# Three of seven own products of a pair as float32r parts, in a three-layer graph network on one core

## The chip, the cores and the metric

The kernel runs on one core of a Trainium2 chip. The metric is the device time of one execution in microseconds (us). Before the change it is 458.73 us, the median of three runs (457.68 to 459.39). "Slower" and "faster" are against that median.

## The reference, cut to what matters

```
h = relu(layernorm(x));  xs = [h]
for W, b in ((W0, b0), (W1, b1), (W2, b2)):        # three layers
    m = concat(h[dst], h[src] - h[dst]) @ W + b    # 80,000 edges
    h = relu(segment_sum(m, dst) / max(count, 1))  # 2,500 nodes, 256 columns
    xs.append(h)
out = x + concat(xs) @ Wf + bf
```

The sum over edges can be written with a matrix A of edge counts between nodes. With W = (Wt over Wb), a layer is relu of h·(Wt − Wb) + share·A·(h·Wb) + b, up to a scaling of each row by its count. The first term is called the *own* term here: it takes a node's own row of h and no edge. A second stream adds h·Wf, layer by layer, to the output, which is kept in `acc`.

## The kernel before, in words

**Layer 0** builds A from the edges, group by group of 504 nodes (486 in the fifth), uses it at once and stores it to memory as bf16 (`a_dram0` to `a_dram4`, by transfers of POOL's queue). Its own products are already made from three float32r parts: a float32 number is split into a high part and a low part of 12 bits each, and a third part across them; three products of float32r parts give the product of two float32 numbers. `Forms` splits a weight (steps high, low, across, last), `Split` and `split_own` split node values.

**Layers 1 and 2** have two phases each. First come ten *nodes* steps: h·Wb and h·Wf for two tiles of 128 nodes, again by three float32r parts; `parts` writes the result in a high and a low float32r half (`zh`, `zl`), `combine` and `sums` make four sums of it for the second phase (`sh`, `sl`), and `add_to_acc` adds the Wf part to `acc`. The fifth group (`Alone`) is multiplied beside them. Then comes the *stream*. The four other groups form two pairs, `Pair(l, 0)` and `Pair(l, 1)`. For a pair, the product of a 2×2 arrangement of blocks is made with seven products instead of eight. The seven right sides are `b11`, `b21`, `b22` and the sums `r1 = b11 + b12`, `r2 = r1 + b22`, `r3 = b11 − r2`, `r4 = r2 + b21`. The 20 tiles of A are cut into five *chunks* of four, so a pair is 5 × 7 = 35 *steps*, and a layer's stream is 70 steps, n = 0 to 69. A step is four float32r products of 128x504. I call the chunks of the two pairs chunk 0 to chunk 9.

For every step, `Pair.make` makes a block in float32r from the staged bf16 data: ACT casts `b11`, `b21`, `b22`, `r1`, `r2`; DVE adds `r1` and `r2` in place in bf16 before their casts, and makes `r3` and `r4` itself. The blocks have seven buffers, and `Stream.run` makes a block at most six steps ahead of the step that PE is at. Each chunk's data are two loads of 504 KB on SP's queue into one of four `staged` buffers.

Each of the seven sums in PSUM also gets its own term: one plain float32 product of the seven-products form, with a weight from `ws` (`b11`, `b21`, `r4`) or from the sums `wsum` (`b22`, `r1`, `r2`, `r3`) and with the same right side taken from `hT`. The right sides that are sums are made by `own_sum` in buffers of `tmps` (six). All seven are issued in the last chunk of a pair (`c == Q // 2 - 1`). When a sum is complete, `take` reads it; the last steps write relu of the result to `hT`, which the next layer's nodes read.

The order on each engine is fixed: PEo, DVEo, ACTo, POOLo and SPo keep the order in which the code is written, and each instruction waits by semaphore only for what it needs. So `tick(n)` and the loops in `run` set the order by their step numbers. SP and POOL are queues of their own: a transfer is issued when its own wait is over, whatever step the other engines are at, but not before the transfers ahead of it in its queue.

Names of the text: `acc` (output), `bf_sb` (bf in all partitions), `add_bf` (called at each `r2` that is made, first in chunk 0 of layer 1), `load_alone` (the loads of the fifth group), `coming` (the forms of the next layer's weights).

Of the kernel before, what the change touches and what calls it, by code (L numbers as in the profile page):

```python
# [298 lines left out]
def by_windows(ctx: ExitStack, tc: tile.TileContext, x, src, dst, Ws, bs, Wf, bf, out, missing):  # L299
# [3 lines left out]
    P = 128  # L303
# [694 lines left out]
    def flat(l):  # L998
        return raws[l].rearrange("p c t d -> p c (t d)") if l < L else wfs[l]
# [42 lines left out]
    own_forms, own_parts, bf_sb, blocks = [], {}, [], []  # L1042

    def forms_of_own():
        parts = [hot.tile([P, DC, D], F32R, name=f"own_w{k}", bufs=1) for k in range(3)]
# [39 lines left out]
    class Group:  # L1085
# [32 lines left out]
    def begin():  # L1118
        g = len(now)
        now.append(Group(g, as_[g]))  # L1120
        if g == 0:
            ps.append(ps_right)
            pre.close()
            apools.append(second.enter_context(tc.tile_pool(name="apool1", bufs=1)))
        if g + 1 < NG:
            as_[g + 1] = new_a(g + 1)
            return
        second.close()
        raw_pools.append(ctx.enter_context(tc.tile_pool(name="raw", bufs=1, side="right")))
        bf_sb.append(raw_pools[-1].tile([P, D], F32, name="bf_sb"))  # L1130
        SPo.dma_start(bf_sb[0], bass.AP(tensor=bf.tensor, offset=bf.offset, ap=[[0, P], [1, D]]))
        blocks.append(ctx.enter_context(tc.tile_pool(name="ready", bufs=7, side="right")))

    def each(of):
# [16 lines left out]
    def take_next(it=iter(range(len([b for b in windows if b[0] == 0]), len(windows)))):  # L1151
# [11 lines left out]
        "h": each((late_final, (q,)) for q in LATE),  # L1163
    }
    later = """
        g d d d B18 u G4 u B23 d d u u G2 u B21 d u B24 ws c e e e e B14 B22 B20 b L3 u d d d b b d u u u c d y
        e e o e o b u b c o o e e u e e w e f b c u u b b d e e e e u c b b d d u u u d w e e e e u c d e d d u
        b b c r g u e u e b w e u u c w b b e y e e e d u u p x u u u c d u u u o e e b b f c e e e b b d o p e
        e e e u u u c d d d u u u o u o b e e b e e c e d b b d u d d r g c e u u u e e y u b b u u u c d d u u
        p u u u b e e e c b y d d b b e o f u c b e e o u e u e e e e u u p d c o d o e e e e b c e e e f d b d  # L1170
        b u u u c b b p r b g u u u u c x u o u u e b b o u u u e c e e e e e e p e o x b b e e e u u u c u u b
        b e c e e o e u b s y b c e e e e u e f k v v v v u u l u r g u s u u u u u u p u q o q o u s p u u o u
        q u u q u u u o u u u n n n n h s h x r l
        """
    acts.update(steps)
    for name in (order + later).split():
# [7 lines left out]
    bf_sb = bf_sb[0]  # L1184
    first_layer.close()

    turn_of = [0, 0]
# [8 lines left out]
    def any_bank():  # L1196
# [74 lines left out]
    class Pair:  # L1271

        def __init__(self, l, i):
            self.l, self.i = l, i
            self.one, self.two = (slice(c0, c0 + n) for c0, n in map(group_of, pairs[i]))
            self.bank, self.r = {}, {}
# [7 lines left out]
        def make(self, c, what, st, made):  # L1284
            to = made[what] = block()[:, :, :GS]
            b11, b21, b12, b22 = (st[:, g, h::2, :] for g in range(2) for h in range(2))
            if what[0] == "b":
                ACTo.copy(to, {"b11": b11, "b21": b21, "b22": b22}[what])
            elif what == "r1":
                DVEo.tensor_add(b12, b11, b12)  # L1290
                ACTo.copy(to, b12)
            elif what == "r2":
                DVEo.tensor_add(b22, b12, b22)
                ACTo.copy(to, b22)
            elif what == "r3":
                DVEo.tensor_sub(to, b11, b22)
            else:
                DVEo.tensor_add(to, b22, b21)

        def own_sum(self, i):  # L1300
# [10 lines left out]
            elif i == 3:  # L1311
                r["r4"] = tmp()[:, :GS]
                DVEo.tensor_add(r["r4"], r["r2"], hT[:, 1, one])

        def multiply(self, c, part, what, made):
            if c == 0:
                self.bank[what] = any_bank()[:, :GS]
            to = self.bank[what]
            if c == Q // 2 - 1:
                if part[0] == "x":  # L1320
                    w = ws[self.l][0][:, part[2], part[1] * P:(part[1] + 1) * P]
                else:
                    w = wsum[:, part[1], :]
                m = {"b11": hT[:, 0, self.one], "b21": hT[:, 1, self.one], "b22": hT[:, 1, self.two]}.get(what)
                PEo.matmul(to, w, self.r[what] if m is None else m, start=False, stop=False)
# [82 lines left out]
    class Stream:  # L1408
# [21 lines left out]
        def run(self, tick):  # L1430
            for n, (m, p, c, part, what, made) in enumerate(self.steps):
                self.make(n + LEAD + 1)
                if c == 2:
                    p.own_sum([w for _, w in SEVEN].index(what) - 2)
# [14 lines left out]
    for l in range(1, L):  # L1449
        order = orders[l]  # L1450
        lone = Alone(l, order)
        if l == 1:
            load_alone(0, order)
            split(order[2])
        pending = []
        stream = Stream(l)
        for i in range(Q + LAG):
            if 0 < i <= Q:
                lone.make(i - 1)
            if i < Q:  # L1460
# [12 lines left out]
            if 0 < i <= DC:  # L1473
                lone.own(i - 1, 0)
            if i >= LAG:
                lone.multiply(i - LAG)
            if i == Q - 1:
                load_alone(Q // 2 - 1, order)
                stream.load(3)
        stream.make(2)  # L1480
        lone.end()
        turn_of[1] = 0
        if l + 1 < L:
            load_b(l + 1, SPo)
            load_wb(l + 1, SPo)
            load_wt(l + 1, SPo)
        load_wf(l + 1, SPo)
        after = orders[l + 1]

        def tick(n):  # L1490
            if n == 68 and l + 1 == L:
                begun.append(split_in_blocks(6, False))
            if n == 3:
                combine(wsum, ws[l][0].rearrange("p c (o n) -> p (c o) n", o=2))
            if n == 40 and l + 1 < L:
                DVEo.tensor_sub(ws[l + 1][0], ws[l + 1][0], ws[l + 1][1])
            if n in (49, 56):
                split(after[(n - 49) // 7])
            if n == 63 and l + 1 < L:
                load_alone(0, after)  # L1500
            if n in ((65,) if l + 1 < L else (63, 65)):
                split(after[2 + (65 - n) // 2])
            if n == 64:
                raw = flat(l + 1)
                coming[:] = [Forms(raw, [raw[:, c, :] if l + 1 < L else raws[L][:, c, 0, :] for c in range(DC)])]
                coming[0].high()
                coming[0].low()
            if n == 66:
                coming[0].across()
            if n == 67:  # L1510
                coming[0].last()

        stream.run(tick)

# [76 lines left out]
```

## Time and profile before

| what | value |
|---|---|
| median of 3 runs | 458.73 us (457.68 to 459.39) |
| profiled execution, its own time | 458.63 us |
| its span, first to last instruction | 456.5 us |
| PE busy | 449.2 us, 98% |
| DVE busy | 372.8 us, 82% |
| ACT busy | 318.9 us, 70% |
| granted clock | 1.000 |

The profile is of one execution. Layer 0 is the first 187 us of the span, layer 1's nodes run to about 236 us and its stream to about 312 us, layer 2's nodes to about 361 us and its stream to about 437 us; the last 20 us are h·Wf of layer 2 and the output. In rows of the profile "PEld" is the load of a weight, which overlaps products. A float32 product stands as two records, a float32r product as one. All ordered instructions have the helper's line 267, so groups are told apart by tile names.

### The profile page before, as it was taken

How to read it: one execution, taken by the hardware profiler on the slowest of the kernel's cores; microseconds unless marked ns; L12 is line 12 of the kernel's file. 1: busy time of each engine (PE TensorE's matmuls, PEld its weight loads, DVE VectorE, ACT ScalarE, POOL GpSimd, SP SyncE). 2: the span in 40 equal slices, each digit the busy share in tenths (PEclk: the TensorE clock that was granted, in tenths of full speed). 3: DMA queues.
4: the chain of work that ended last, by engine and by line, in shares of the span. 5: the costliest groups of instructions: out<-in, count | busy, mean ns of one | idle time of the engine just before them, and what ended most of it. 6: DMA issues, size and time to landing. Idle time of an engine off the chain costs nothing.

```text
span 456.5 us, 7452 instructions
## 1 busy us (share of the span) xinstructions
PE 449.2 (98%) x2737; PEld 358.2 (78%) x2737; DVE 372.8 (82%) x724; ACT 318.9 (70%) x586; POOL 43.6 (10%) x64
## 2 busy tenths in 40 slices
PE   8999999999999999999999999999999999999996
PEld 4888877888888888878878868867888787688685
DVE  6999999998899555379979859876999687569796
ACT  5898878777764535397779849756877897497540
POOL 4790101101022010100000000000000000000000
PEclk9999999999999999999999999999999999999999
DMA  8310266833719985611495522011124855220015
GB/s 277 115 36 1 51 122 111 157 79 70 151 36 192 154 199 103 145 47 45 123 378 204 182 90 93 0 45 47 46 54 142 326 184 180 90 92 1 1 53 176
DMA packets 22056, 52.47 MB, mean 115 GB/s; under 512 B 1931, under 2 KB 12382, under 8 KB 22014
## 3 DMA queue, kind: packets, MB, share of 16 engines
q1 hardware_dynamic: 14654, 33.83, 22.2%
q0 software_dynamic: 5856, 16.48, 19.0%
q10 hardware_dynamic: 1504, 1.63, 1.1%
q8 instruction: 22, 0.36, 0.3%
q14 instruction: 20, 0.16, 0.1%
HBM read 36.47 MB, written 15.62 MB: 114 GB/s over the span
## 4 chain that ended last, share of the span: by engine, by line
PE 89%; DMA 3%; POOL 3%; DVE 3%; ACT 1%; issue 1%; ACTq 0%; POOLq 0%
PE bank L267 89%; DMA acc<-in_x_dram 2%; POOL acc L267 1%; DMA staged<-a_dram 1%; DVE st L267 1%; POOL es L267 1%; POOL ed L267 1%; DVE acc L267 0%; DVE staged L267 0%; DVE mv L267 0%; ACT block L267 0%; DVE tmp L267 0%; ACT tmp L267 0%; DVE zl L267 0%; ACT zh L267 0%
## 5 line engine op out<-in xcount | busy, mean ns | idle before, releaser
L267 ACT CAST block<-staged 128x1008 fp32r<-128x1008 bf16 x120 | 117.9, 1031 | 18.9 <-DVE staged L267 6.5
L267 PE MATMUL bank<-block,zh 128*128 128x504 f32 (+1 forms) x200 | 83.7, 418 | 0.0
L267 PE MATMUL bank<-a,zh 128*128 128x504 f32 (+1 forms) x200 | 80.3, 401 | 0.0
L267 PE MATMUL bank<-a,zl 128*128 128x504 f32 (+1 forms) x200 | 77.9, 389 | 0.0
L267 PE MATMUL bank<-block,zl 128*128 128x504 f32 (+1 forms) x200 | 77.2, 386 | 0.0
L267 ACT CAST a<-bank 128x480 fp32r<-128x480 f32 (+1 forms) x105 | 53.0, 568 | 26.6 <-PE bank L267 26.6
L267 PE MATMUL bank<-block,sh 128*128 128x504 f32 x160 | 69.1, 432 | 0.0
L267 DVE TENSOR_TENSOR one_m<-iota_m,key_m 128x2048 bf16<-128x2048 bf16 (+2 forms) x55 | 63.9, 1162 | 5.9 <-PE bank L267 5.9
L267 PE MATMUL bank<-block,staged 128*128 128x512 f32 (+1 forms) x288 | 62.8, 369 | 0.2 <-DVE staged L267 0.2
L267 PE MATMUL bank<-block,sl 128*128 128x504 f32 x160 | 62.5, 391 | 0.0
L267 PEld LDWEIGHTS bank<-block,staged 128*128 128x128 f32 x288 | 49.3, 189 | 10.6 <-DVE staged L267 0.8
L267 DVE TENSOR_TENSOR block<-staged 128x1008 fp32r<-128x1008 bf16 x40 | 46.9, 1204 | 5.3 <-PE bank L267 3.9
L267 PEld LDWEIGHTS bank<-block,zh 128*128 128x128 f32 x200 | 37.6, 188 | 10.8 <-issue 2.1
L267 PEld LDWEIGHTS bank<-block,zl 128*128 128x128 f32 x200 | 37.6, 188 | 10.5 <-issue 3.5
L267 PEld LDWEIGHTS bank<-a,zl 128*128 128x128 f32 x200 | 37.7, 188 | 7.4 <-issue 0.5
L267 PEld LDWEIGHTS bank<-a,zh 128*128 128x128 f32 x200 | 37.6, 188 | 7.5 <-issue 0.5
L267 DVE TENSOR_TENSOR one_n<-iota_n,key_n 128x640 bf16<-128x640 bf16 (+2 forms) x110 | 42.7, 429 | 0.0
L267 PEld LDWEIGHTS bank<-block,sh 128*128 128x128 f32 x160 | 30.1, 188 | 10.5 <-issue 3.5
L267 PEld LDWEIGHTS bank<-block,sl 128*128 128x128 f32 x160 | 30.1, 188 | 9.3 <-issue 3.7
L267 DVE TENSOR_TENSOR staged<-staged 128x1008 bf16<-128x1008 bf16 x40 | 27.1, 679 | 12.0 <-ACT block L267 11.6
L267 PEld LDWEIGHTS <-one_m 128*128 128x128 bf16 x834 | 29.1, 98 | 7.3 <-issue 4.3
L267 PE MATMUL bank<-own_w,hT 128*128 128x256 f32 x144 | 34.7, 385 | 0.0
(192 smaller groups left out, 645.2 us busy)
## 6 DMA issues: line engine op xcount, KB each, us to landing
staged<-a_dram SPq DMA_DIRECT2D x52, 504.0 KB
a_dram<-a POOLq DMA_DIRECT2D x20, 630.0 KB, 9.0
acc<-in_x_dram POOLq DMA_DIRECT2D x3, 640.0 KB, 17.2
out_dram<-acc SPq DMA_DIRECT2D x5, 256.0 KB
acc<-in_x_dram SPq DMA_DIRECT2D x2, 512.0 KB
acc<-in_x_dram ACTq DMA_DIRECT2D x1, 768.0 KB
out_dram<-acc SPq DMA_DIRECT2D x5, 128.0 KB
wt<-in_L_gnn_W_dram SPq DMA_DIRECT2D x2, 256.0 KB
```

The lines of the kernel that those rows point to most:

```text
L267: return self.tc.keep_in_program_order(call(*args, **kwargs))
```

## The change

Four things change, in layers 1 and 2.

1. `b11`, `b21` and `r4` get their own term as three float32r products: `own_high` (ACT) and `own_rest` (DVE) split the right side into three `tmps` buffers, and a `Forms` splits the layer's weight into one of the four `staged` buffers (`room`). The other four own products stay plain float32.
2. All own products leave the last chunk where the table `AT` says so: in pair 0, `b22` goes to chunk 1, `b11` and `b21` to chunk 2, `r4` to chunk 3; in pair 1, `b21` goes to chunk 2, `b11` and `r4` to chunk 3. `r1`, `r2`, `r3` (and `b22` in pair 1) stay in the last chunk. The steps at which sums, splits, forms and loads for the next layer are issued move with it; `coming` is begun at step 54 instead of 64 and takes three of the seven block buffers from then on.
3. `r1` is written back to memory in layer 1 (ten transfers of SP's queue, 252 KB each), and layer 2 reads it, so it leaves ten adds of DVE out.
4. `bf` is added by four transfers of POOL's queue that add to `acc`, instead of by four adds of DVE. The load of `bf_sb` falls away.

```
     def add_bf():
+        row = bass.AP(tensor=bf.tensor, offset=bf.offset, ap=[[0, P], [0, 5], [1, D]])
         for t in range(0, NT, 5):
-            DVEo.tensor_add(acc[:, t:t + 5, :], acc[:, t:t + 5, :], bf_sb.unsqueeze(1).to_broadcast([P, 5, D]))
+            POOLo.dma_start(acc[:, t:t + 5, :], row, accum_op=OP.add)
             yield
             yield
...
+    THREE = ("b11", "b21", "r4")
+    OWNS = THREE + ("b22", "r1", "r2", "r3")
+    AT = {
+        "own": ((2, 2, 3, 1, 4, 4, 4), (3, 2, 3, 4, 4, 4, 4)),
+        "sums": ((14, 16, 20, 17), (50, 51, 55, 51)),
+        "high": ((0, 0, 20), (39, 45, 56)),
+        "rest": ((3, 10, 23), (41, 47, 57)),
+        "wsum": 2, "forms": (6, 8, 9, 9), "split": (53, 57, 65, 64), "load": 61,
+        "sub": 39, "coming": (54, 61, 64, 65), "begun": 68,
+    }
...
             elif what == "r1":
-                DVEo.tensor_add(b12, b11, b12)
+                if self.l == 1:
+                    DVEo.tensor_add(b12, b11, b12)
+                    SPo.dma_start(a_dram[pairs[self.i][1]][:, 4 * c:4 * c + 4:2, :], b12)
                 ACTo.copy(to, b12)
...
+        def own_high(self, what):
+            self.threes[what] = [tmp()[:, :GS].bitcast(F32R) for _ in range(3)]
+            ACTo.activation(self.threes[what][0], self.own_of(what), AF.Copy, scale=DOWN)
+
+        def own_rest(self, what):
+            h = self.own_of(what)
+            high, low, across = self.threes[what]
+            DVEo.tensor_sub(low, h, high.bitcast(F32))
+            DVEo.scalar_tensor_tensor(across, low.bitcast(F32), -E12, high.bitcast(F32), op0=OP.mult, op1=OP.add)
+
+        def own(self, to, part, what):
+            if what in self.threes:
+                for k, m in enumerate(self.threes.pop(what)):
+                    PEo.matmul(to, own_forms[-1].parts[k][:, part[2], part[1] * P:(part[1] + 1) * P], m,
+                               start=False, stop=False)
...
-            if c == Q // 2 - 1:
-                if part[0] == "x":
...
+            if c == AT["own"][self.i][OWNS.index(what)]:
+                self.own(to, part, what)
...
         def tick(n):
...
+            if n == AT["wsum"]:
                 combine(wsum, ws[l][0].rearrange("p c (o n) -> p (c o) n", o=2))
+                room = stage.tile([P, 4 * GS], F32R, name="staged")
+                own_forms.append(Forms(ws[l][0], [ws[l][0][:, c, :] for c in range(DC)],
+                                       [room[:, k * DC * D:(k + 1) * DC * D].rearrange("p (c d) -> p c d", c=DC)
+                                        for k in range(3)]))
+            for k, step in enumerate(("high", "low", "across", "last")):
+                if n == AT["forms"][k]:
+                    getattr(own_forms[-1], step)()
```

On PE, where the own product of `b11` stands in the last chunk of pair 0 of layer 1 before:

```order
L267 MATMUL bank<-hT,wt 128x504
L267 MATMUL bank<-block,zh 128x504
L267 MATMUL bank<-block,zl 128x504
L267 MATMUL bank<-block,zh 128x504
L267 MATMUL bank<-block,zl 128x504
L267 MATMUL bank<-hT,wt 128x504
```

And now, in chunk 2 of the same pair (`staged` is here the buffer with the split weight):

```order
L267 MATMUL bank<-tmp,staged 128x504 x3
L267 MATMUL bank<-block,zh 128x504
L267 MATMUL bank<-block,zl 128x504
L267 MATMUL bank<-block,zh 128x504
L267 MATMUL bank<-block,zl 128x504
L267 MATMUL bank<-tmp,staged 128x504 x3
```

One float32 row became three rows of float32r, and the place is two chunks earlier.

On ACT, at the end of chunk 0's casts and through chunk 1's, layer 1. Before:

```order
L267 CAST block_3305<-staged_3256 128x2x504
L267 CAST block_3325<-staged_3259 128x2x504
L267 CAST block_3332<-staged_3259 128x2x504
L267 CAST block_3342<-staged_3259 128x2x504
L267 CAST block_3349<-staged_3259 128x2x504
L267 CAST block_3357<-staged_3259 128x2x504
L267 CAST block_3380<-staged_3262 128x2x504
L267 CAST block_3386<-staged_3262 128x2x504
```

Now (`staged_3342` is `room`, `staged_3254`, `_3257` and `_3260` are chunks 0, 1 and 2):

```order
L267 CAST block_3304<-staged_3254 128x2x504
L267 ACTIVATE tmp_3309<-hT_86 128x504
L267 ACTIVATE tmp_3313<-hT_86 128x504
L267 CAST block_3332<-staged_3257 128x2x504
L267 CAST block_3343<-staged_3257 128x2x504
L267 CAST block_3352<-staged_3257 128x2x504
L267 CAST block_3359<-staged_3257 128x2x504
L267 CAST block_3368<-staged_3257 128x2x504
L267 ACTIVATE staged_3342<-wt_2828 128x512
L267 CAST block_3394<-staged_3260 128x2x504
L267 ACTIVATE staged_3342<-wt_2828 128x256 x4
L267 CAST block_3407<-staged_3260 128x2x504
```

Two high parts went between the casts of chunk 0 and chunk 1, and five instructions on the weight between those of chunk 1 and chunk 2. The first write to `room` also waits for the store of chunk 0's `r1`, since `room` takes chunk 0's buffer.

On SP's queue, from the loads of chunk 2 on, layer 1 now:

```order
L267 DMA staged_3260<-a_dram1_108 128x2016
L267 DMA brow_95<-in_L0_gnn_b2_dram 1x256
L267 DMA wbf_3292<-in_L0_gnn_W2_dram 128x2x256
L267 DMA wt_3293<-in_L0_gnn_W2_dram 128x2x256
L267 DMA wbf_3292<-in_L0_gnn_Wf_dram 128x2x256
L267 DMA a_dram1_108<-staged_3254 128x2x504
L267 DMA staged_3324<-a_dram0_107 128x2016
L267 DMA staged_3324<-a_dram1_108 128x2016
L267 DMA a_dram1_108<-staged_3257 128x2x504
```

The rows are the same before, but for the two stores to `a_dram1`: a store of `r1` stands ahead of each later chunk's loads.

More of the change, by code (lines that the diff above doesn't have):

```diff
@@ L1040, in last @@
                 ACTo.activation(self.parts[2][:, c, :], self.rest[c], AF.Copy, scale=1.0 / C1)
-    own_forms, own_parts, bf_sb, blocks = [], {}, [], []
+    own_forms, own_parts, blocks = [], {}, []
     def forms_of_own():
@@ L1129, in begin @@
         raw_pools.append(ctx.enter_context(tc.tile_pool(name="raw", bufs=1, side="right")))
-        bf_sb.append(raw_pools[-1].tile([P, D], F32, name="bf_sb"))
-        SPo.dma_start(bf_sb[0], bass.AP(tensor=bf.tensor, offset=bf.offset, ap=[[0, P], [1, D]]))
         blocks.append(ctx.enter_context(tc.tile_pool(name="ready", bufs=7, side="right")))
@@ L1165, in by_windows @@
     later = """
[L1166 to L1173, printed above, removed]
+        g d d d B18 u G4 u B23 d d u u G2 u B21 d u B24 ws c e e e e B14 B22 B20 b L3 u d d d b b d u u u c d y e e o e o b u b c o o e e u e e w e f b c u u b b d e e e e u c b b d d u u u d w e e e e u c d e d d u b b c r g u e u e b w e u u c w b b e y e e e d u u p x u u u c d u u u o e e b b f c e e e b b d o p e e e e u u u c d d d u u u o u o b e e b e e c e d b b d u d d r g c e u u u e e y u b b u u u c d d u u p u u u b e e e c b y d d b b e o f u c b e e o u e u e e e e u u p d c o d o e e e e b c e e e f d b d b u u u c b b p r b g u u u u c x u o u u e b b o u u u e c e e e e e e p e o x b b e e e u u u c u u b b e c e e o e u b s y b c e e e e u e f k v v v v u u l u r g u s u u u u u u p u q o q o u s p u u o u q u u q u u u o u u u n n n n h s h x l r
         """
@@ L1183, in by_windows @@
     ps_left = ctx.enter_context(tc.tile_pool(name="ps_left", bufs=4, space=PSUM))
-    bf_sb = bf_sb[0]
     first_layer.close()
@@ L1275, in __init__ @@
             self.one, self.two = (slice(c0, c0 + n) for c0, n in map(group_of, pairs[i]))
-            self.bank, self.r = {}, {}
+            self.bank, self.r, self.threes = {}, {}, {}
         def load(self, c):
@@ L1313, in own_sum, with own_of @@
                 DVEo.tensor_add(r["r4"], r["r2"], hT[:, 1, one])
+        def own_of(self, what):
+            m = {"b11": hT[:, 0, self.one], "b21": hT[:, 1, self.one], "b22": hT[:, 1, self.two]}.get(what)
+            return self.r[what] if m is None else m
+        def own_high(self, what):
[11 more added lines that the diff above has]
+                               start=False, stop=False)
+            elif part[0] == "x":
+                PEo.matmul(to, ws[self.l][0][:, part[2], part[1] * P:(part[1] + 1) * P], self.own_of(what),
+                           start=False, stop=False)
+            else:
+                PEo.matmul(to, wsum[:, part[1], :], self.own_of(what), start=False, stop=False)
         def multiply(self, c, part, what, made):
@@ L1318, in multiply @@
             to = self.bank[what]
-            if c == Q // 2 - 1:
-                if part[0] == "x":
[L1321 to L1325, printed above, removed]
+            if c == AT["own"][self.i][OWNS.index(what)]:
+                self.own(to, part, what)
             for k, j in enumerate((2 * c, 2 * c + 1)):
@@ L1432, in run @@
                 self.make(n + LEAD + 1)
-                if c == 2:
-                    p.own_sum([w for _, w in SEVEN].index(what) - 2)
+                for k in range(4):
+                    if n == AT["sums"][p.i][k]:
+                        p.own_sum(k)
+                for k, own in enumerate(THREE):
+                    if n == AT["rest"][p.i][k]:
+                        p.own_rest(own)
+                    if n == AT["high"][p.i][k]:
+                        p.own_high(own)
                 p.multiply(c, part, what, made)
@@ L1490, in tick @@
         def tick(n):
-            if n == 68 and l + 1 == L:
+            if n == AT["begun"] and l + 1 == L:
                 begun.append(split_in_blocks(6, False))
-            if n == 3:
+            if n == AT["wsum"]:
                 combine(wsum, ws[l][0].rearrange("p c (o n) -> p (c o) n", o=2))
-            if n == 40 and l + 1 < L:
+                room = stage.tile([P, 4 * GS], F32R, name="staged")
[5 more added lines that the diff above has]
+                    getattr(own_forms[-1], step)()
+            if n == AT["sub"] and l + 1 < L:
                 DVEo.tensor_sub(ws[l + 1][0], ws[l + 1][0], ws[l + 1][1])
-            if n in (49, 56):
-                split(after[(n - 49) // 7])
-            if n == 63 and l + 1 < L:
+            if n == AT["load"] and l + 1 < L:
                 load_alone(0, after)
[L1501 to L1511, printed above, removed]
+            for k in range(3 if l + 1 < L else 4):
+                if n == AT["split"][k]:
+                    split(after[k])
+            for k, step in enumerate(("high", "low", "across", "last")):
+                if n == AT["coming"][k]:
+                    if k == 0:
+                        raw = flat(l + 1)
+                        coming[:] = [Forms(raw, [raw[:, c, :] if l + 1 < L else raws[L][:, c, 0, :] for c in range(DC)])]
+                    getattr(coming[0], step)()
         stream.run(tick)
```

## The prediction

> **What bounds the kernel now.** First the page: who is busy, and on whom the chain of waits lies. Then the chain in order of time.
>
> ```profile
> span 456.5 us, 7452 instructions
> PE 449.2 (98%) x2737; PEld 358.2 (78%) x2737; DVE 372.8 (82%) x724; ACT 318.9 (70%) x586; POOL 43.6 (10%) x64
> ...
> PE 89%; DMA 3%; POOL 3%; DVE 3%; ACT 1%; issue 1%; ACTq 0%; POOLq 0%
> ```
>
> ```profile
> 200.00 252.10 PE bank L267 x1094
> 452.10 0.02 issue
> 452.12 0.48 DVE acc L267
> ```
>
> ```profile
> PEld bank L267 <- ACT block L267: 1.5, 8, 0.2
> ```
>
> From 200.00 to 452.10 us the chain is PE alone. Both streams that change lie in it, so a microsecond of PE taken out is one off the end, unless a new wait takes its place. The third view (waits) says how close that is: in the whole run PE's weight loads waited for ACT's casts 8 times, 1.5 us together.
>
> **The own product.** The timeline of PE over the last chunk of pair 0 in layer 1, then layer 0's own products, which are already three float32r parts:
>
> ```profile
> 262.31 1.01 PE L267 MATMUL bank<-hT,wt 128*128 128x504 f32 x2
> ...
> 272.85 1.00 PE L267 MATMUL bank<-tmp,wt 128*128 128x504 f32 x2
> ...
> 274.16 0.39 PE L267 MATMUL bank<-block,zh 128*128 128x504 f32 x1
> ...
> 275.98 0.39 PE L267 MATMUL bank<-block,zh 128*128 128x504 f32 x1
> ```
>
> ```profile
> 96.45 0.62 PE L267 MATMUL bank<-wt,own_w 128*128 128x504 f32 x2
> 96.91 0.39 PE L267 MATMUL bank<-own_h,own_w 128*128 128x504 f32 x1
> ```
>
> Durations overlap, so starts are what counts. Between 274.16 and 275.98 lie 8 float32r products: 0.228 us each, 0.91 a step. Between 262.31 and 272.85 lie 6 steps with an own product: 1.757 each, so a float32 own product costs 0.847. Three float32r products cost 0.68 (by layer 0's rows, 0.46 for two, 0.69). Each replaced product saves 0.16, and there are 3 × 4 pairs = 12: **1.9 us**. The Trainium skill ("FP8 and Floating Point Precision", TensorE Precision Notes) has true FP32 as four passes through the array and reduced precision as one read. By that a quarter of 0.847 would go, 0.21 each or 2.5 us; the rows show each float32r product at 0.228 rather than 0.212, so I keep 1.9 and make the rule a rival.
>
> **What DVE and ACT get.** Groups of both, ACT's first:
>
> ```profile
> L267 ACT CAST block<-staged 128x1008 fp32r<-128x1008 bf16 x120 | 117.9, 1031 | 18.9 <-DVE staged L267 6.5 <-PE bank L267 6.4 <-DVE tmp L267 2.3
> L267 ACT ACTIVATE wt<-hT 128x504 fp32r<-128x504 f32 x6 | 3.7, 624 | 5.2 <-issue 2.6 <-PE bank L267 1.9 <-DVE hT L267 0.6
> L267 ACT ACTIVATE own_w<-wt 128x512 fp32r<-128x512 f32 x1 | 0.7, 653 | 0.0
> L267 ACT ACTIVATE own_w<-wt 128x256 fp32r<-128x256 f32 x4 | 1.5, 450 | 0.7 <-DVE wt L267 0.7
> L267 ACT COPY tmp<-bank 128x504 f32<-128x504 f32 x8 | 4.6, 578 | 16.0 <-PE bank L267 16.0
> L267 ACT ACTIVATE hT<-hT 128x1008 f32<-128x1008 f32 x8 | 8.3, 1044 | 4.4 <-DVE hT L267 4.4
> ```
>
> ```profile
> L267 DVE TENSOR_TENSOR block<-staged 128x1008 fp32r<-128x1008 bf16 x40 | 46.9, 1204 | 5.3 <-PE bank L267 3.9
> L267 DVE TENSOR_TENSOR staged<-staged 128x1008 bf16<-128x1008 bf16 x40 | 27.1, 679 | 12.0 <-ACT block L267 11.6
> L267 DVE TENSOR_TENSOR hT<-bank,tmp 128x504 f32<-128x504 f32 x12 | 8.1, 678 | 6.4 <-PE bank L267 6.4
> L267 DVE TENSOR_TENSOR acc<-acc,bf_sb 128x1280 f32<-128x1280 f32 x4 | 5.9, 1486 | 0.0
> L267 DVE TENSOR_TENSOR wt<-hT,wt 128x504 fp32r<-128x504 f32 x6 | 4.1, 680 | 0.9 <-ACT wt L267 0.9
> L267 DVE SCALAR_TENSOR_TENSOR wt<-own_w,wt 128x256 f32<-128x256 f32 x2 | 0.8, 422 | 0.0
> ```
>
> Per layer ACT gains six high parts (0.62 each) and a weight split (0.65 + 4 × 0.45): 6.2 us. DVE gains 12 × 0.68 for the rests and 4 × 0.42 for the weight: 9.8 us; it loses the four bf adds (5.9) in layer 1 and ten `r1` adds (6.8) in layer 2. None of that is on the chain; it costs only where a cast comes late. Four tight places:
>
> *Start of a stream.* A chunk is 6.4 us of PE.
>
> ```profile
> 237.28 5.69 ACT L267 CAST block<-staged 128x1008 fp32r<-128x1008 bf16 x6
> 243.15 6.83 ACT L267 CAST block<-staged 128x1008 fp32r<-128x1008 bf16 x7 [0.17 <-DVE staged L267]
> ```
>
> ```profile
> 243.93 2.33 DVE L267 TENSOR_TENSOR block<-staged 128x1008 fp32r<-128x1008 bf16 x2
> ```
>
> Six casts take 5.69, so 0.95 each and 4.75 a chunk: 1.65 spare. Chunks 0 to 2 get 1.25 + 2.45 = 3.7 of new ACT work against 3 × 1.65 = 5.0 spare, and 0.85 + 2 × 0.68 of own products now stand there for PE to work on. The two high parts push chunk 1's first cast from 237.28 + 3 × 0.95 = 240.1 to about 241.2; PE is at step 2 when the first of those three casts ends (238.3) and wants step 7 at 242.9. Chunk 1's casts then end near 246.4. The weight follows: its high part to 247.1, DVE's low parts behind chunk 1's two blocks (246.3 before, 247.6 with a rest of 1.36 ahead) to 248.4, ACT and DVE across to 249.5, ACT's last to 249.9. PE reaches step 14 at 238.3 + 12 × 0.91 + 0.85 = 250.1 and wants the last part two products on, at 250.6. No wait, 0.7 to spare; and the high part could start 1.3 later (0.6 of it before DVE is free): its limit is about 247.7.
>
> *The store ahead of `room`.* The weight's high part also waits for chunk 0's `r1` store, which stands behind three chunks' loads and the next layer's weights.
>
> ```profile
> 224.00:228.00 4.00, 4.00 (x19) 3.35 (x18) 3.80 (x9) 2.98 (x5) 0.00 (x0) 1.00 0.67 194
> 228.00:232.00 4.00, 4.00 (x19) 3.33 (x19) 2.87 (x7) 2.01 (x4) 0.00 (x0) 1.00 0.99 372
> 232.00:236.00 4.00, 4.00 (x18) 3.09 (x17) 3.85 (x9) 2.93 (x4) 0.00 (x0) 1.00 0.98 370
> 236.00:240.00 4.00, 4.00 (x17) 2.80 (x16) 2.51 (x3) 3.76 (x6) 0.00 (x0) 1.00 1.06 391
> ```
>
> (Stretches of layer 1; the last two columns are the transfers' busy share and GB/s.) Seven loads of 0.52 MB and three weights of 0.26 are 4.4 MB: by these rates done at 237.7. The engines are full here, and two bf transfers now come into it, because POOL issues each when its five tiles of `acc` have their last add:
>
> ```profile
> 222.59 0.87 DVE L267 SCALAR_TENSOR_TENSOR acc<-bank,share,acc 128x256 f32<-128x256 f32 x2
> ...
> 231.73 0.87 DVE L267 SCALAR_TENSOR_TENSOR acc<-bank,share,acc 128x256 f32<-128x256 f32 x2
> ```
>
> Tiles 14 and 15 are ready at 222.59, 16 and 17 at 227; 18 and 19 just after 231.73. So the third transfer starts near 223 and the fourth near 233 (the first two fall where loads are few). The nearest price is an adding transfer of x:
>
> ```profile
> 184.00:188.00 4.00, 4.00 (x19) 3.38 (x18) 0.00 (x0) 0.90 (x2) 0.61 (x1) 1.00 0.99 145
> ```
>
> ```profile
> acc<-in_x_dram POOLq DMA_DIRECT2D x3, 640.0 KB, 17.2
> ...
> acc<-in_x_dram POOLq DMA_DIRECT2D x1, 512.0 KB, 6.7
> ```
>
> At 145 GB/s, 0.66 MB holds the engines 4.5 us; at the 200 of stretches with no ramp it would be 3.3. Two of them move the loads' end to 244.3 to 246.7, the store (0.26 MB) lands at 245.5 to 248.5, and the limit for the weight is 247.7: a stall of 0 to 0.8 us in layer 1, which I take as **0.2**. Chunk 0's loads end at 230 now and may slip to 237 before the cast of `b22` (237.3) is late. Layer 2 has no store and no bf.
>
> *Three staged buffers instead of four.* `room` holds one until PE's step 62, so a chunk's load begins when the chunk three ahead of it is made, some 13 us before need; 1.03 MB at 370 take 2.8, the `r1` store before it 1 to 2. Hidden. If it were not, a chunk would stall by the whole excess.
>
> *Last chunk of pair 0.* It loses four own products, 3.4 us of PE, which covered `take`. It is now 6.4 + 3 × 0.85 = 8.9 us of PE, against ACT's 4.75 + 2 × 0.58 + 2 × 1.04 = 8.0 and DVE's 8 × 0.68 + 2 × 0.68 + 2 × 1.20 = 9.2. DVE is the fuller one, but blocks are made up to six steps ahead (5.5 us) and the next chunk gives 0.9 back. I take nothing; with that cover gone it costs up to 1 us a layer.
>
> `r1`'s stores, the earlier forms of the next layer and the missing `bf_sb` load are covered by the same spare time: 0.
>
> **Sum**, against the profiled execution's own 458.63 (0.10 below the median): 458.63 − 1.9 + 0.2 = **456.9**.
>
> **Rivals.** *B, more comes out*: a float32r product costs a quarter of a float32 one (the skill's passes, above), or the own products moved to the streams' starts also fill part of the 1.5 us of waits. 458.63 − 2.5 = **456.1**. For it: `b22`'s product now stands in chunk 1. Against: the starts of float32r products, 0.228 apart everywhere, and that the waits fall in chunk 0, ahead of it.
>
> *C, given back*: DVE late in pair 0's last chunk, or the weight late by the store. Decides if DVE cannot hide 9.2 in 8.9, twice. 1.3 us over both layers: 456.9 + 1.3 = **458.2**. For it: DVE was busy 82% in the mean, and its work grows by 4 to 10 us. Against: the adds that fall away.
>
> *D, slower*: the bf transfers do not share, they displace. Where POOL's stores ran beside one small SP load (bf_sb), from 169 to 172 us:
>
> ```profile
> q0 software_dynamic: 128, 0.56, 92.6%
> q1 hardware_dynamic: 124, 0.13, 14.8%
> ```
>
> SP got 19% of the bytes. With landings of 8.4 us (6.7 × 640/512) each, SP moves 19% of some 330 GB/s from 224 to 241, 1.06 MB instead of 5; chunk 0's second half (1.55 MB in all with the fifth group's load) ends at 242.3 instead of 230, 5.0 past the 237.3 of its cast: 456.9 + 5.0 = **461.8** (rounded). It decides from a slip of 7 us on. For it: the third bf transfer starts with chunk 0's loads. The Trainium skill ("DMA: Bandwidth & Descriptors", SWDGE vs HWDGE vs iDMA) has each engine take turns between the two kinds of queue; by turns of 1 KB against 4 KB packets SP would keep most of its bytes, which speaks against D, and the rows above agree only half, POOL's packets there being 5 KB. That the split does not happen at all is out: order shows three rows.
>
> **How the numbers follow.** A 0.58, B 0.14, C 0.18, D 0.10. A's own range is 456.2 to 457.6 (12 × 0.21 or 0.157, stall 0 to 0.8). The range for 8 in 10 takes in B and C: 455.6 to 459.6. About 0.5% (2.3 us) is what a measurement here tells from no change: faster is below 456.4, slower above 461.0. Faster: a quarter of A and nearly all B, 0.28. Slower: D, 0.09. Within: 0.63.
>
> **What would show it.** Right: 36 products `bank<-tmp,staged` 0.23 apart, own steps of 1.59; streams shorter by 0.95 us each; waits of PE for casts still near 1.5 in all; the store of chunk 0 landed before 247. Wrong: a gap on PE at step 14 in layer 1 (weight late), at the first steps of chunk 5 (DVE late), or at step 2 (loads late), or a chain that leaves PE between 200 and 450.

## The result, and the profile after

The change makes the kernel slower: 462.95 us (median of 6 runs, 461.45 to 464.46) against 459.06 us (6 runs beside them); the ratio is 1.0098, with a 95% interval from 1.008 to 1.0116. Forecast were 456.9 us and a range up to 459.6. Rival D (bf transfers displace loads, 461.8) is the nearest.

The profiled execution has a span of 461.2 us, 4.7 more than before. Its page, and under it four pieces of its chain of waits in order of time (start, length, what; both in us):

```profile
span 461.2 us, 7558 instructions
PE 449.7 (98%) x2749; PEld 361.4 (78%) x2749; DVE 380.7 (83%) x742; ACT 328.0 (71%) x608; POOL 48.8 (11%) x68
...
PE 87%; DMA 6%; POOL 2%; ACT 1%; DVE 1%; issue 1%; ACTq 0%; SPq 0%; POOLq 0%
```

```profile
31.91 192.73 PE bank L267 x1570
...
227.28 11.81 DMA staged<-a_dram
...
239.15 12.67 DMA a_dram<-staged
...
254.67 201.32 PE bank L267 x888
```

The chain leaves PE once, between 224.64 and 254.67 us, at the start of layer 1's stream. Two transfers carry it there: the first load of chunk 1, issued at 227.28 and landed at 239.1, and chunk 0's `r1` store, which SP's queue issued only then, at 239.15, and which landed at 251.8. PE's busy share, 98% as before, shows none of this. The waits do (who <- whom: us in total, times, longest):

```profile
PEld bank L267 <- ACT block L267: 4.9, 12, 1.7
PEld bank L267 <- ACT staged L267: 2.7, 3, 1.1
ACT staged L267 <- DMA a_dram<-staged: 3.9, 1, 3.9
```

The first row was 1.5 us in 8 waits before. Its growth comes from the two loads of chunk 0, one for each of the pair's groups. The casts of `b11` and `b21` need the first load, DVE's add for `r1` needs the second. When ACT and DVE began with them, before and in the change:

```profile
234.14 1.96 ACT L267 CAST block<-staged 128x1008 fp32r<-128x1008 bf16 x2
234.88 0.68 DVE L267 TENSOR_TENSOR staged<-staged 128x1008 bf16<-128x1008 bf16 x1
```

```profile
235.95 1.97 ACT L267 CAST block<-staged 128x1008 fp32r<-128x1008 bf16 x2 [2.40 <-DMA staged<-a_dram]
237.27 0.69 DVE L267 TENSOR_TENSOR staged<-staged 128x1008 bf16<-128x1008 bf16 x1 [2.99 <-DMA staged<-a_dram]
```

So these loads landed at 235.9 and 237.2. The other two rows of waits are new: ACT could not write the weight's high part into `room` for 3.9 us, because the store that reads this buffer had not landed, and PE then waited three times for the weight's parts. PE at this place (start, us, operation, count, and in brackets its idle time and releaser):

```profile
251.60 0.38 PE L267 MATMUL bank<-block,zl 128*128 128x504 f32 x1
252.52 0.49 PE L267 MATMUL bank<-tmp,staged 128*128 128x504 f32 x1 [0.54 <-ACT staged L267]
253.76 0.49 PE L267 MATMUL bank<-tmp,staged 128*128 128x504 f32 x1 [0.75 <-ACT staged L267]
254.67 0.72 PE L267 MATMUL bank<-tmp,staged 128*128 128x504 f32 x1 [0.41 <-ACT staged L267]
255.19 0.62 PE L267 MATMUL bank<-block,zh 128*128 128x504 f32 x1
255.61 0.62 PE L267 MATMUL bank<-block,zl 128*128 128x504 f32 x1
...
258.39 0.39 PE L267 MATMUL bank<-block,zl 128*128 128x504 f32 x1
258.62 0.40 PE L267 MATMUL bank<-block,zh 128*128 128x504 f32 x1
```

From 251.60 to 254.67 are 3.07 us for three products that take 0.69 without a wait: 2.4 us. Behind them the products are 0.42 us apart instead of 0.23 until 258.1. That is the clock:

```profile
252.00:254.00 2.00, 0.73 (x2) 0.37 (x2) 1.02 (x3) 2.00 (x4) 0.00 (x0) 1.00 0.68 250
254.00:256.00 2.00, 1.58 (x4) 1.09 (x4) 1.97 (x5) 1.81 (x5) 0.00 (x0) 0.69 0.03 9
256.00:258.00 2.00, 2.00 (x6) 1.61 (x5) 1.46 (x3) 2.00 (x3) 0.00 (x0) 0.50 0.92 266
```

(Busy time of PE, PEld, DVE, ACT and POOL in each stretch, then the granted clock, the transfers' share and GB/s.) The clock was 0.50 for some 3.4 us (1.2 of the second stretch, all of the third, and 0.2 behind it); nine products at 0.19 more are 1.7 us.

Layer 2, where none of this happens, shows what the change is worth by itself:

```profile
379.60 0.86 PE L267 MATMUL bank<-tmp,staged 128*128 128x504 f32 x3
380.29 0.39 PE L267 MATMUL bank<-block,zh 128*128 128x504 f32 x1
...
381.21 0.84 PE L267 MATMUL bank<-tmp,staged 128*128 128x504 f32 x3
```

A step with an own product takes 1.61 us (379.60 to 381.21) against 1.757 before: 0.147 saved, 12 times, 1.8 us. Whole streams say a little less: from its first product to its last, layer 2's takes 75.23 us, and 76.08 before, so 0.85 a layer and 1.7 us in all.

The account of the profiled execution. The waits of weight loads overlap the product that PE is at, so the late casts are counted on PE itself: from 234.30, the last products ahead of the stream, to 240.16, in the stream's third step, are 5.86 us; before, the same products took 3.71 (234.98 to 238.69). That is 2.2 us, less than the 4.9 − 1.5 = 3.4 of the waits.

```profile
234.98 1.79 PE L267 MATMUL bank<-hT,wt 128*128 128x486 f32 x4
...
238.69 0.39 PE L267 MATMUL bank<-block,sl 128*128 128x504 f32 x1
```

```profile
234.30 1.79 PE L267 MATMUL bank<-hT,wt 128*128 128x486 f32 x4
237.04 0.50 PE L267 MATMUL bank<-block,zh 128*128 128x504 f32 x1 [0.94 <-ACT block L267]
...
239.83 0.49 PE L267 MATMUL bank<-block,sh 128*128 128x504 f32 x1 [0.68 <-ACT block L267]
240.16 0.39 PE L267 MATMUL bank<-block,sl 128*128 128x504 f32 x1
```

Late casts 2.2, late weight 2.4, slow clock 1.7, own products −1.7: 4.6. The span grew by 4.7. Two differences outside the streams nearly cancel in it: PE of before waited twice for DVE just ahead of 200.00, in the stage of nodes, 0.7 us that this execution did not have, and the end, from the last add to the last instruction, took 4.7 us instead of 3.9.

### The profile page after: what moved, and what is told of

Read it like the earlier page. It is cut to its first block, busy times and chain, and to the rows that moved or that the text cites. A ratio compares the mean times of both kernels' runs of the same rounds, so it can differ in the third digit from the quotient of the medians.

```text
span 461.2 us, 7558 instructions
## 1 busy us (share of the span) xinstructions
PE 449.7 (98%) x2749; PEld 361.4 (78%) x2749; DVE 380.7 (83%) x742; ACT 328.0 (71%) x608; POOL 48.8 (11%) x68
## 4 chain that ended last, share of the span: by engine, by line
PE 87%; DMA 6%; POOL 2%; ACT 1%; DVE 1%; issue 1%; ACTq 0%; SPq 0%; POOLq 0%
PE bank L267 87%; DMA a_dram<-staged 3%; DMA staged<-a_dram 3%; POOL acc L267 1%; DMA dst_i<-in_dst_dram 1%; POOL es L267 1%; POOL ed L267 0%; ACT block L267 0%; ACT zh L267 0%; DVE pick L267 0%; DVE acc L267 0%; ACT staged L267 0%; DVE st L267 0%; DVE behind L267 0%; ACT iota_n L267 0%
## 5 line engine op out<-in xcount | busy, mean ns | idle before, releaser
L267 PE MATMUL bank<-block,zh 128*128 128x504 f32 (+1 forms) x200 | 79.3, 396 | 0.9 <-ACT block L267 0.9
L267 PEld LDWEIGHTS bank<-block,sh 128*128 128x128 f32 x160 | 30.1, 188 | 11.5 <-issue 2.8
L267 DVE TENSOR_TENSOR staged<-staged 128x1008 bf16<-128x1008 bf16 x30 | 20.4, 680 | 15.3 <-ACT block L267 12.0
```

Of the source, the lines that this page charges most:

```text
L267: return self.tc.keep_in_program_order(call(*args, **kwargs))
```

## The experiments

Three theories at first. **Theory 1**: the bf transfers fill the DMA engines, make chunk 0's loads late and, through them and the queue, its store and the weight. **Theory 2**: the store ahead of `room` makes the weight late by itself. **Theory 3**: ACT and DVE have too much to do at the stream's start. Theory 4, on the clock, came with the late weight.

**bf back on DVE.** The rest of the change stays.

```diff
-            POOLo.dma_start(acc[:, t:t + 5, :], row, accum_op=OP.add)
+            DVEo.tensor_add(acc[:, t:t + 5, :], acc[:, t:t + 5, :], bf_sb.unsqueeze(1).to_broadcast([P, 5, D]))
```

> Theory 1, the bf transfers fill the DMA engines from 224 to 249 us and so make chunk 0's loads late (about 2.4 us of waits), and by the queue also its r1 store and the weight that waits for it (2.6 us, then about 1.7 us at half the clock): with bf back on DVE all of it goes, and the own products' 1.9 us come out: 456.5 us (456 to 457.5). Theory 2, the store ahead of room makes the weight late whatever bf does: the 2.4 of the loads go, the 4.3 at step 14 stay: about 460.5. Theory 3, ACT and DVE have too much at the stream's start: the gap at step 14 stays, and DVE, which gets 5.9 us of bf adds back, makes it longer: 461 or more.

Measured: 458.01 us, ratio to before 0.9975 (0.996 to 0.999). Its waits, its chain, and the rows of ACT and PE around the weight:

```profile
PEld bank L267 <- ACT block L267: 2.2, 11, 0.2
```

```profile
32.10 417.89 PE bank L267 x2566
```

```profile
248.38 0.76 ACT L267 ACTIVATE staged<-wt 128x256 fp32r<-128x256 f32 x2 [0.16 <-DVE wt L267]
```

```profile
249.89 0.86 PE L267 MATMUL bank<-tmp,staged 128*128 128x504 f32 x3
```

From 32.10 to the end the chain is PE alone; the weight's last part is ready at 249.14, 0.75 us before the three own products begin and 1.2 before the third of them, which reads it; there is no wait for it. The store is still there, as are all of ACT's and DVE's new operations and four DVE adds on top. Theories 2 and 3 fall: neither the store nor the engines' work makes the weight late without the bf transfers. The gain is 1.1 us by the medians, and 458.01 lies outside the 456 to 457.5 expected; its interval (0.5 to 1.8 us) just holds the 1.7 that the two streams save (75.23 and 75.21 us here). In the profile the end behind the last add takes 4.6 us, 0.7 more than before; why, the runs do not show.

**No `r1` store.** bf stays on the transfers; layer 2 adds `r1` again.

```diff
-                if self.l == 1:
-                    DVEo.tensor_add(b12, b11, b12)
-                    SPo.dma_start(a_dram[pairs[self.i][1]][:, 4 * c:4 * c + 4:2, :], b12)
+                DVEo.tensor_add(b12, b11, b12)
```

> The r1 store of layer 1 is taken out and r1 is added again in layer 2; the bf transfers stay. Theories 1 and 2 both have room free as soon as chunk 0 is cast (about 242.5), so the gap at step 14 and the slow clock behind it go (4.3 us), while the late loads stay: about 458.7 us. Theory 3: no change at step 14, and DVE has ten more adds of 0.68 in layer 2: 463 or more.

Measured: 459.75 us, ratio 1.0004 (0.9985 to 1.0024), 3.2 us below the change by the medians and 1.1 above the 458.7 expected. Its chain of waits has no weight in it; the late casts stay, longer than expected:

```profile
PEld bank L267 <- ACT block L267: 5.9, 12, 2.8
```

So the store is the link between the bf transfers and the weight: without either one, the gap at step 14 is not there.

**The kernel before, with the bf transfers alone.**

```diff
-            DVEo.tensor_add(acc[:, t:t + 5, :], acc[:, t:t + 5, :], bf_sb.unsqueeze(1).to_broadcast([P, 5, D]))
+            POOLo.dma_start(acc[:, t:t + 5, :], row, accum_op=OP.add)
```

> The kernel before with nothing changed but bf, added by the four transfers. Theory 1: chunk 0's loads are late here too, 2.4 us (a little more, since PE has no own products and no weight to wait for at the start): 461 us, slower by 0.5%. Theories 2 and 3 lay the loss on the store or on the new work of ACT and DVE, neither of which is here: 458.5 to 459, unchanged.

Measured: 462.29 us, ratio 1.006 (1.0043 to 1.0077), about 2.8 us slower by the ratio and 3.2 by the medians (461 us was expected).

```profile
PEld bank L267 <- ACT block L267: 4.4, 9, 2.0
```

The waits for casts go from 1.5 to 4.4 us with nothing else changed but the load of `bf_sb`, which falls away. The transfers alone are enough to make a kernel slower whose stream has neither `room` nor a store. (PE's chain began 1.7 us later in this profile, at 33.57, so its span says less than its waits.)

**The transfers later,** behind the first rest of pair 1 in layer 1, all four at once.

```diff
+        late = raw_pools[-1].tile([P, 1], F32, name="late")
+        POOLo.tensor_copy(late, behind[:, :1])
-        for t in range(0, NT, 5):
+        for t in (15, 0, 5, 10):
             POOLo.dma_start(acc[:, t:t + 5, :], row, accum_op=OP.add)
```

> The change with its four bf transfers held back by a small POOL copy that waits for the first rest of pair 1 (step 41 of layer 1's stream, near 275 us), the group of tiles that layer 2 needs first in front. Theory 1: no waits at the stream's start, the store of chunk 0 lands near 240, and the transfers find room for 47 us of landings before layer 2's first adds: 456.6 us (455.8 to 457.5). Theory 2: gap at step 14 stays, 460.5. If the transfers displace loads wherever they stand, the waits move to chunks 8 and 9 or to layer 2's nodes: 459 to 461.

Measured: 478.87 us, ratio 1.0424 (1.0388 to 1.046). The expectation failed by 22 us, and in the direction of its last sentence, only larger. Two pieces of the chain, and the queues from 310 to 318 us (packets, MB, share of the 16 engines' time):

```profile
287.84 17.28 DMA a_dram<-staged
...
307.93 11.52 DMA a_dram<-staged
```

```profile
q0 software_dynamic: 616, 0.61, 100.0%
q1 hardware_dynamic: 208, 0.21, 9.7%
```

An `r1` store of 252 KB took 17.28 us beside the four transfers and the next 11.52, and the splits for layer 2 waited for the staged buffers that these stores held. In 8 us POOL's queue kept the engines full with 0.61 MB: 8 × 16 / 616 = 0.208 us for a packet of 1 KB. In the kernel before, x's adding transfers moved 595 packets of 1 KB in 96.6% of the engines' time from 184 to 188 us: 0.104. So it is not the place alone that is wrong but the transfer's price.

**What sets that price.** Two versions of the transfer in its own place. One reads rows of x, so as many packets of the same size from different addresses (its output has rows of x where bf belongs):

```diff
-            POOLo.dma_start(acc[:, t:t + 5, :], row, accum_op=OP.add)
+            POOLo.dma_start(acc[:, t:t + 5, :], xr[:, 0:5, :], accum_op=OP.add)
```

> The change with rows of x as the source of the four transfers in place of the one row of bf (so the output has x's rows added where bf belongs): still 640 packets of 1 KB each, but from 640 different addresses. In the kernel before, x's own adding transfers took 0.104 us a packet (595 packets in 96.6% of 4 us on 16 engines). Theory a (number of packets): as the change, 463 us. Theory b (one row read by all): 0.104 us a packet, 66 engine-us, landing in 5 to 8 us; the loads are about half as late and the store of chunk 0 lands before 248: 458.5 to 460. Theory c: 463.

The other reads five copies of bf in one row of 5 KB:

```diff
+        SPo.dma_start(bf5[0], bass.AP(tensor=bf.tensor, offset=bf.offset, ap=[[0, 1], [0, 5], [1, D]]))
-        row = bass.AP(tensor=bf.tensor, offset=bf.offset, ap=[[0, P], [0, 5], [1, D]])
+        row = bf5[0].to_broadcast([P, 5, D])
```

> The change, its four transfers in their places, but their source is a row of five copies of bf in DRAM (1280 values, written once near 170 us), so that a partition's 5 KB can be one packet. In the change's trace a bf transfer is 640 packets of 1 KB at 0.16 to 0.17 us each, some 105 engine-us; the stores of counts with 5 KB a packet took 0.35 us each. Theory a, the number of packets is the price: 128 x 0.35 = 45 engine-us, landing in 4 to 7 us; the loads at the start are hardly late and the weight is in time: 458 to 459 us. Theory b, the price is that 128 partitions read one and the same row: landings stay near 12 us, 461 to 463. Theory c, any transfer of POOL's queue holds SP's back whatever its packets: unchanged, 463.

Measured: rows of x 457.97 us, ratio 0.9973 (0.9954 to 0.9992); the row of 5 KB 457.24 us, ratio 0.9958 (0.9942 to 0.9975). Each alone takes the whole loss away. POOL's queue from 202 to 208 us, where the first transfer runs nearly alone, in the change, with rows of x, and with the row of 5 KB:

```profile
q0 software_dynamic: 461, 0.47, 76.5%
```

```profile
q0 software_dynamic: 652, 0.65, 74.5%
```

```profile
q0 software_dynamic: 128, 0.57, 48.4%
```

Of 96 engine-us (6 us of 16 engines) the packets took 73.4, 71.5 and 46.5: 0.159 us for one KB of the one row, 0.110 for one KB of different rows, 0.363 for five KB of one row. A whole transfer is 640 × 0.159 = 102, 640 × 0.110 = 70 or 128 × 0.363 = 46 engine-us. And in the crowded stretch, 232 to 240 us, everything that moved, in the change and with rows of x:

```profile
DMA packets 891, 2.31 MB, mean 288 GB/s; under 512 B 75, under 2 KB 403, under 8 KB 890
q1 hardware_dynamic: 546, 1.96, 76.7%
```

```profile
DMA packets 1088, 3.00 MB, mean 375 GB/s; under 512 B 111, under 2 KB 426, under 8 KB 1087
q1 hardware_dynamic: 839, 2.75, 87.1%
```

SP's queue moved 1.96 MB against 2.75, and a KB of it held an engine for 50 ns (76.7% of 128 us) against 41. The only difference between the two kernels is what POOL's packets read, 640 rows of x or 640 times one row of bf, so the source is the cause: the same packets from different rows cost what the prediction took from x, and then the start of the stream has no more waits than with bf on DVE (2.2 us for casts in both, none for the weight). The store of chunk 0 landed at 247.0 us there, where the prediction has 245.5 to 248.5. Theory b has this run nearly as forecast (457.97 against 458.5 to 460). The row of 5 KB came out as theory a had it, though (457.24 against 458 to 459): 128 reads of one row are few enough. So a alone and b alone are each half of it; what costs is many small reads of the same place, and either remedy is enough. Theory c (POOL's queue holds SP's back whatever it moves) falls.

Why repeated reads of a row are slow the runs do not show. One row of x was not tried as the source, so that the repetition is slow, and not the place where bf lies, is argued and not shown. For it speaks the kernel before: its load of `bf_sb` reads the same row of bf 128 times without adding, and from 169 to 172 us its 124 packets took 14.8% of 48 engine-us, 0.057 us each.

**The clock.** With bf on DVE, the weight is split three steps later, and in a second kernel four to five:

```diff
-        "forms": (6, 8, 9, 9)
+        "forms": (9, 11, 12, 12)        # and, in the second, (11, 13, 13, 13)
```

> The change with bf on DVE, and the split of layer 1's and 2's weight moved three steps later on ACT and DVE (from steps 6, 8, 9, 9 to 9, 11, 12, 12; nothing else). With bf on DVE its last part came 0.8 us before PE wanted it; three steps are 2.7 us, so PE stalls about 2 us at step 14 in each layer: 458.0 + 4 = 462. Theory 4, PE's clock falls to half when PE has idled some 2.5 us of about 3.4 and stays low for 3 to 6 us: with 2 us of stall the clock stays at 1.00 (or falls in one layer at most). If any stall at this place takes the clock down, it is near 0.7 around 255 here too.

> The same with the split at steps 11, 13, 13, 13: about 3.5 to 4.5 us of stall a layer. Theory 4: the clock falls to 0.5 some 3.3 to 4.8 us after PE went idle and stays there for 3 to 6 us in each layer, which costs 1.5 to 2.5 us on top of each stall: 458.0 + 8 + 4 = 470. Without the clock's part 466.

Measured: 460.76 us (ratio 1.0040, 1.0023 to 1.0057) with 3.5 us of waits for the weight over both layers, and 464.0 us (1.0107, 1.0071 to 1.0142) with 5.2. The stalls were shorter than expected, above all in layer 2 (the weight had 1.2 us to spare, not the 0.8 reckoned with). But the clock stayed at 1.00, also behind the longer stall of layer 1, in which PE was idle for nearly all of 252 to 254 us:

```profile
252.00:254.00 2.00, 0.10 (x1) 0.10 (x1) 1.20 (x4) 1.50 (x3) 0.00 (x0) 1.00 0.03 10
254.00:256.00 2.00, 1.59 (x6) 1.11 (x7) 2.00 (x4) 0.91 (x3) 0.00 (x0) 1.00 0.00 0
```

Theory 4 as it stood, a length of stall from which the clock falls, is refuted by that. Two theories were left, and three single executions were made for them: the change twice more, and the last kernel once more.

> The change once more, for the clock alone. In its first profile the clock was 0.50 from 255 to 258 us, behind three waits of 2.7 us together within 3.4 us; with the weight made late on purpose, 3.4 us of waits within 3.7 left it at 1.00. Theory 4a, the clock is judged in windows that run freely of the program, and the same stall takes it down in one execution and not in another: about an even chance of a drop here, and without one some 1.7 us less in the stream of layer 1 (78.3 instead of 79.9 us from its first product to its last). Theory 4b, the shape of the stall decides (two single float32r products between three waits): a drop in every execution of the change.

> The same a third time. 4a: about an even chance. 4b: a drop near 255 us again.

> The kernel with the weight split at steps 11, 13, 13, 13 once more. 4a: an even chance of a drop behind layer 1's stall of 3.4 us. 4b: no drop.

Measured: 464.95, 463.72 and 463.32 us. The clock in the stretches behind the stall: the change's second and third execution, then the late weight's second:

```profile
256.00:258.00 2.00, 1.77 (x4) 1.09 (x5) 1.97 (x5) 1.82 (x4) 0.00 (x0) 0.54 0.16 50
```

```profile
256.00:258.00 2.00, 1.59 (x7) 1.08 (x8) 1.97 (x5) 1.81 (x5) 0.00 (x0) 1.00 0.06 21
```

```profile
254.00:256.00 2.00, 2.00 (x8) 1.59 (x7) 2.00 (x4) 1.03 (x1) 0.00 (x0) 0.65 0.00 0
256.00:258.00 2.00, 2.00 (x6) 1.56 (x5) 1.90 (x4) 0.11 (x1) 0.00 (x0) 0.50 0.44 71
```

A drop, none, and a drop: the change fell in two of three executions, and the late weight, with the same waits to 0.02 us, in one of two. The execution of the change without a drop had the longest waits for the weight of the three (3.3 us against 2.7 and 3.0), and ran on the same chip as the second. Theory 4b (the stall's shape decides) falls on both sides, and 4a, that the same stall takes the clock down in one execution and not in another, is what is left. From the first to the last product of layer 1's stream the two executions of the late weight took 78.3 us without the drop and 79.9 with it: 1.6 us. The change took 78.9 without it, where 78.3 was expected, its stall being longer, and 79.9 twice with it.

The Trainium skill ("TensorE: Matmul & The Clock Gate", What's actually happening) has the gate look at windows of 3.4 us that run freely of the program. The traces agree with that length: a slow stretch lasts 3.4 us (1.4 and 2.0 in the last two rows), and with the transfers later there were two, of 10.2 and 6.8 us, three and two times as long. That the place of the windows decides is argued, not shown. In the 3.4 us ahead of the three slow stretches PE was still busy for 1.7 to 1.8 us, so none of them followed 3.4 us without a product.

The fastest version is the change with bf from the row of 5 KB: 457.24 us, 0.42% below before. (With bf on DVE it is 0.25%, and the two intervals overlap.) Its chain leaves nothing to take from the transfers:

```profile
32.11 417.90 PE bank L267 x2566
```

## Why the prediction was wrong, point by point

- **What bounds the kernel.** Right: with the waits gone, the chain is PE alone from 32.1 to 450.0 us, the last product, and what PE loses or gains there decides. Of the 1.7 us that the streams lost, the medians with bf on DVE show 1.1.
- **The own product.** Right in mechanism, a little large: 0.147 for each replaced product against 0.16, since three float32r products of parts stand 0.69 to 0.70 us long. A stream is 0.85 us shorter instead of 0.95, 1.7 us in all instead of 1.9. Rival B's quarter (0.21) did not come.
- **Start of a stream.** The reckoning of ACT and DVE was right: in the kernel with bf on DVE and the store in place, the weight's last part was ready 1.2 us before the product that reads it, forecast 0.7. Layer 2 had no wait.
- **The store ahead of `room`.** This step failed, and with it the forecast. The place, the order in the queue and the limit (247.7 us) were right. (PE came to step 14 at 251.8 instead of 250.1, so the limit became 249.4, and the high part began 2.4 us behind it.) The term that fell is "At 145 GB/s, 0.66 MB holds the engines 4.5 us", a price from x's adding transfer. With x's rows as source that price held (0.110 us a packet against 0.104) and the stall did not come. With the one row of bf a transfer cost 102 engine-us, 6.4 us of all 16, and SP's packets beside it went slower too: the two moved the end of the loads ahead of the store from 237.7 not to 244.3 to 246.7 but to 251.0. The store was issued at 239.15, behind the late first load of chunk 1 (at 235.1 with bf on DVE), and landed at 251.8 instead of 245.5 to 248.5. The stall was 2.4 us instead of 0 to 0.8, and the clock added 1.7. The late casts, 2.2 us, were not in the sum at all. The prediction gave a limit for the last load of chunk 0 alone ("may slip to 237"), and that load, at 237.2, nearly kept it; the first load, which the casts of `b11` and `b21` need at 234.1, landed at 235.9. The prediction had looked at how much the two transfers moved and at what such a transfer cost, but not at what they read.
- **Three staged buffers; the last chunk of pair 0; the remaining edits at 0.** Right: no wait at any of them with bf on DVE or from the row of 5 KB. Rival C's first half (DVE late) fell. Its second half (the weight late by the store) came, but only together with the bf transfers, and with 2.4 us in layer 1 alone.
- **Rival D.** Its place and direction were right, its reason half: transfers on POOL's queue do not displace SP's loads as such (the rows of x), these did. Its 5.0 us lay on the loads alone; measured were 2.2 there, and 4.1 for the weight and the clock, to which it gave nothing. So it is luck that its 461.8 (its terms add up to 461.9) came near. At 0.10 it had too small a chance: the row that priced the transfer was of another source, and that was reason to widen the range.
- **What would show it.** A gap at step 14 and at step 2, and a chain that leaves PE, were named as signs of error, and all three came.

## What to carry to other kernels

Price a transfer by one with the same source pattern, not only the same size and operation: a broadcast from one small row was nearly half as dear again per packet as the same bytes from different rows, and dearer still with four at once. A row made long enough for one packet a partition cost less than half. And where a buffer is handed on from a store to an engine's write, follow what the store waits behind: a delay of the loads came back later as a second, larger one.

## What was not expected of the hardware

- A packet of 1 KB that adds into SBUF took 0.159 us when all read one row, 0.110 from different rows, and 0.208 with several such transfers at once; SP's queue then had 9.7% of the engines' time, and a store of 252 KB took 11.5 to 17.3 us.
- After a stall of PE of 2.4 to 3.1 us the granted clock fell to 0.50 for some 3.4 us in three of five executions, with the same kernels showing both; it cost 1.6 us in a pair of executions with equal waits.
